# Layer 1 of the first image in the other stream, beside layer 0 of the second, with TensorE in order of emission

## The chip, the cores and the metric

The kernel runs on one core of a Trainium2 chip. The metric is the device time of one execution in microseconds, lower is better; where several runs are named, their median stands for them.

The engines, as the profile names them: PE is TensorE's matrix multiplication, PEld its loading of weights, DVE is VectorE, ACT is ScalarE, POOL is GpSimd, SP is SyncE, which here only issues transfers. ACT and POOL issue transfers too.

## The reference, cut to what matters

Four images of 48 channels and 256 x 256 pixels, in float32, go through four layers. Each layer normalises its input by groups of three channels and adds its result to its input (`_gn` is that normalisation):

```python
x = x + _L0_conv_ref(_gn(x), ...)   # 1x1 conv to 288, 3x3 depthwise conv, q*k in the spectrum of 8x8 patches,
                                    # layer norm over 96 channels, times v, 1x1 conv to 48
x = x + _L1_conv_ref(_gn(x), ...)   # 1x1 conv to 288, a filter in the spectrum of 8x8 patches, 3x3 depthwise conv,
                                    # gelu(first half) * second half, 1x1 conv to 48
x = x + _L2_conv_ref(_gn(x), ...)   # running sums over the image; two 3x3 convs give each pixel a box;
                                    # four bilinear look-ups in the sums, divided by the area
x = x + _L3_conv_ref(_gn(x), ...)   # 1x1 conv to 192, 3x3 depthwise conv, gelu * gate, 1x1 conv to 48,
                                    # a filter in the spectrum of 8x8 patches
```

The images don't depend on each other. Within an image a layer needs the whole of the layer before, because the statistics of the normalisation run over the image.

## The kernel before

**Two streams.** `Net.run` (L1354) holds two lists of jobs, a and b. A job is a generator that emits the instructions of one layer of one image piece by piece and yields a number after each piece, its cost in units of its own. `advance` takes the next piece from the stream whose sum of costs (`at`) is smaller, so the instructions of the two streams are emitted in turns. (n,i) is layer n of image i.

- a: the statistics of image 0, then (0,0), (1,0), (0,1), (1,1), (0,2), (1,2), (0,3), (1,3), then (3,0), (3,1), (3,2), (3,3).
- b: `patch_weights` (the matrices of layer 1), `taps` (the weights of layer 3), the statistics of images 1 to 3, then (2,0), (2,1), (2,2), (2,3).

A job waits until the layer before it of the same image is emitted in full, layer 1 also for `patch_weights`; the stream's sum is then raised to the time in units at which that was done. A layer 0 yields 1806 units, a layer 1 1425, a layer 2 3220, a layer 3 1080. So (1,0) has no partner: b has nothing to do until (2,0) may start.

**What belongs to a stream.** `self.stream` selects the PSUM banks (`bank`, L224: five of 512 float32 for a, two for b; layer 2 holds the eighth bank for its weights, L983, tag `w4`), the queue of ordinary transfers (`dma`, L227: SP for a, GpSimd for b) and the side of SBUF (`pool`, L234).

**Who sets the order on an engine.** The framework reorders the emitted instructions of an engine as it finds them ready, save those passed through `keep_in_program_order` (`pinned`, L230), which keep their order among each other. Pinned before the change: the first matmul of each group of layer 2 and its work on VectorE, the statistics of layers 0 and 1, and the transfers of layer 1's second and third phase, which are on SP by name whatever the stream.

**Layer 0** (`layer0`, L422) goes through 128 units. A unit is two rows of one half of the image; two units share a strip, for which `columns2` (L283) loads the input in six transfers (two buffers). The work on a unit is spread over several turns of the loop at L558: `convolve` (12 matmuls at L379 and 4 at L387 through `convolve2`, into four banks, evicted by ScalarE at L463), `spectra` (L471; L474, L477), `inverse` (L486, L487, L491), `gate`, `turn` (L524, L526), `project` (L536). Each turn yields twice, 7 units each time.

**Layer 1** (`layer1`, L655) has three phases. In the first it multiplies 16 strips by `win` (L692), 512 matmuls each into a bank of its own, evicts them (three of four on ScalarE at L699, one on VectorE at L697) and writes the result to DRAM as `hD`. In the second it goes through 36 groups of channels: `around` (L744) makes the rims of the patches (L750, into four banks) and sends them through small transfers (`yh` from `yb`, L761), and four times `gated` (L763) multiplies by `wd` and `yh` (L767, L773) into two banks, which L778 and L779 turn into the gated product; it goes to DRAM as `gD`. In the third it turns 16 strips of `gD` round (L844, three banks; evicted at L846), projects them (L856, one bank) and adds the input (L861). It yields 3 units for four matmuls in the first phase, 4 for a `gated` or an `around` in the second, 5 for a quarter of a strip in the third.

**Layer 2** (`layer2`, L961) first makes the running sums (`sums`, L893; L926, L947) and then goes through 32 pieces in four steps each, and one turn more to finish. A step is 16 gathers of GpSimd (L1105) into one of three buffers, the weighing and adding of the gathered values on VectorE (L1117 to L1127), and in turns the convolutions of a later piece (L999, L1008, L1011), its small products (L1024) and the finishing of an earlier one (L1136, L1143). A step yields 22 units. Its columns are loaded through ScalarE's queue (`look`, L1013).

**Layer 3** (`layer3`, L1214) is a loop of 135 turns of 8 units, mostly L379, L387 and L1268.

Of the kernel before, what the change touches and what calls it, by code (L numbers as in the profile page):

```python
# [188 lines left out]
class Net:  # L189
    def __init__(self, ctx, tc, a, out):  # L190
# [6 lines left out]
        self.stream = "a"  # L197
# [26 lines left out]
    def bank(self):  # L224
        return self.banks[self.stream].tile([128, 512], F32, name=self.nm("ps"), tag="ps")

    def dma(self, out, of):  # L227
        (self.nc.sync if self.stream == "a" else self.nc.gpsimd).dma_start(out, of)  # L228

    def pinned(self, instruction):  # L230

        return self.tc.keep_in_program_order(instruction)

# [137 lines left out]
    def convolve2(self, AB, W, n, j, to):  # L371
# [5 lines left out]
        def full(q, b):  # L377
            for g in range(3):
                nc.tensor.matmul(  # L379
                    to(q, b), A[:, j + half * q, 128 * b + g : 128 * b + g + 128], W[:, g, :],  # L380
                    start=b == 0 and g == 0, stop=b == 1 and g == 2,
                )

        def tails(b):
            for q in range(2):
                p = slice(64 * q, 64 * q + 58)
                nc.tensor.matmul(  # L387
                    to(q, b), B[p, j, 128 * b : 128 * b + 128], W[p, 3, :], start=b == 1, stop=b == 0
                )
# [32 lines left out]
    def layer0(self, x, mr, y, xb):  # L422
        nc, a = self.nc, self.a
        st = self.stat.tile([112, 129, 6], F32, name=self.nm("st"), tag="st" + self.stream, bufs=1)
        with ExitStack() as ctx:
# [39 lines left out]
            def spectra(t):  # L465
                t.t = []
                for f, c in ((self.fq, 0), (self.fk, 96)):
                    banks = [self.bank() for _ in range(2)]
                    for h in range(2):
                        p = slice(64 * h, 64 * h + 64)  # L470
                        nc.tensor.matmul(v3(banks[h]), f[p], t.qkv[p, :, c : c + 96], start=True, stop=True)  # L471
# [7 lines left out]
            def inverse(t):  # L479
# [5 lines left out]
                for h in range(2):  # L485
                    nc.tensor.matmul(po[64 * h : 64 * h + 64, 0:384], self.back[:, 0:64], t.t[h][:], start=True, stop=True)  # L486
# [34 lines left out]
            def turn(t):  # L521
                pt = self.bank()
                for b in range(4):
                    nc.tensor.transpose(pt[:96, 128 * b : 128 * b + 128], t.un[:, b, :], self.ident[:])  # L524
# [3 lines left out]
            def project(t, other):  # L528
# [5 lines left out]
                for i, of in ((0, other), (1, t)):  # L534
                    n = 48 if i else 64
                    nc.tensor.matmul(pp[64 * i : 64 * i + n, :], pr[:, 0:n], of.u[:], start=True, stop=True)  # L536
# [118 lines left out]
    def layer1(self, x, mr, y):  # L655
# [4 lines left out]
        with ExitStack() as ctx:  # L660
# [25 lines left out]
            for s in range(NS):  # L686
                xt = xts[s % 3]
                hs = sb.tile([128, 8 * NG, 2, 16], F32, name="hs", tag="hs")
                for b in range(16):
                    for h in range(2):  # L690
                        ps = self.bank()
                        nc.tensor.matmul(  # L692
                            ps[:, :288], xt[64 * h : 64 * h + 49, 128 * b : 128 * b + 128],
                            win[64 * h : 64 * h + 49], start=True, stop=True,
                        )
# [12 lines left out]
        with ExitStack() as ctx:  # L708
# [35 lines left out]
            def around(t):  # L744

                for e in range(4):
                    ps = self.bank()
                    for i in range(2):
                        c = 4 * i + e
                        nc.tensor.matmul(  # L750
                            ps[64 * i : 64 * i + 64, :].rearrange("p (s n) -> p s n", n=32),
                            t.wr[:, 64 * c : 64 * c + 64], t.hg[:, :, c, :], start=True, stop=True,
                        )
# [9 lines left out]
            def gated(t, e):  # L763
                both = [self.bank() for _ in range(2)]
                for i in range(2):
                    c = 4 * i + e
                    nc.tensor.matmul(  # L767
                        both[i][:].rearrange("p (s n) -> p s n", n=32), t.wd[:, 128 * c : 128 * c + 128],
                        t.hg[:, :, c, :], start=True, stop=False,
                    )  # L770
                for i in range(2):
                    p = slice(64 * i, 64 * i + 64)
                    nc.tensor.matmul(  # L773
                        order(both[i][:]), t.wd[p, 1024 + 128 * e : 1152 + 128 * e], pick(t.yh, e)[p],
                        start=False, stop=True,
                    )
# [32 lines left out]
        with ExitStack() as ctx:  # L809
# [25 lines left out]
            def turn(s, j):  # L835
                gs, got = strips[s], []
                for q in range(3):
                    pt = self.bank()
                    for b in range(4):
# [4 lines left out]
                        nc.tensor.transpose(pt[:96, 128 * b : 128 * b + 128], of, self.ident[:])  # L844
# [5 lines left out]
            def project(s, j, got):  # L850
                xt, yt = buffers[s % 2]
                pp = self.bank()
                for last in range(2):
                    for h in range(2):
                        n = 48 if h else 64
                        nc.tensor.matmul(  # L856
                            pp[64 * h : 64 * h + n, :], pr[:, h if last else 2, 0:n], got[2 if last else h][:],
                            start=not last, stop=bool(last),
                        )
# [494 lines left out]
    def run(self, layers=(0, 1, 2, 3)):  # L1354
# [5 lines left out]
        a = [("first", 0)] + [(n, i) for i in images for n in (0, 1) if n in layers] + [(3, i) for i in images if 3 in layers]  # L1360
        b = ([("weights", 0)] if 1 in layers else []) + ([("taps", 0)] if 3 in layers else [])
        b += [("first", i) for i in images[1:]]
# [9 lines left out]
        def advance(f):  # L1372
            self.stream = f
            if now[f] is None:
# [6 lines left out]
                now[f] = self.first_statistics(i) if n == "first" else self.patch_weights() if n == "weights" else self.taps() if n == "taps" else self.layer(n, i)  # L1381
            try:
# [74 lines left out]
```

## Time and profile before

The median of nine runs is 22818.67 us (22727.34 to 22904.18). The profiled execution took 22756.06 us; its span, from first to last instruction, is 22754.3 us, and the mean granted clock of TensorE is 0.854 of full speed.

| | busy us | share of the span | instructions |
|---|---|---|---|
| profiled execution (span 22754.3 us) | | | 227410 |
| PE | 18541.1 | 81% | 79706 |
| PEld | 11053.8 | 49% | 79706 |
| DVE | 10282.4 | 45% | 22561 |
| ACT | 6017.6 | 26% | 12781 |
| POOL | 8473.3 | 37% | 8902 |

Where the jobs lie in the span, read from the stretches in which their lines have instructions:

| us | stream a | stream b |
|---|---|---|
| 0 to 1890 | statistics of image 0, (0,0) | until about 1130: matrices of layer 1, weights of layer 3, statistics of images 1 to 3 |
| 1890 to 3080 | (1,0) | nothing |
| 3080 to 7550 | (0,1), (1,1) | (2,0): sums until about 3480, then gathers |
| 7550 to 12170 | (0,2), (1,2) | (2,1) |
| 12170 to 16750 | (0,3), (1,3) | (2,2) |
| 16750 to 21730 | (3,0), (3,1), (3,2) | (2,3) |
| 21730 to 22754 | (3,3) | nothing |

How to read it: a stretch of the span is printed as its bounds, its length, the busy time and the number of instructions of PE, PEld, DVE, ACT and POOL, the granted clock of TensorE (1.00 is full speed), the mean busy share of the sixteen DMA engines and the GB/s that they moved. A group of instructions is printed with its line, engine, operation and shapes, its count, its busy time in us and the mean ns of one. A float32 matmul stands in the records as two instructions, so 12 matmuls at L379 are 24 records. A wait names who waited, for whom, and the total, the number and the longest in us.

### The profile page before, as it was taken

The page shows a single profiled execution, that of the slowest core. Times are in us where ns is not written, and L with a number is a line of the kernel's source. Part 1 is how long each engine was busy: PE and PEld are TensorE (multiplying, and loading weights), DVE is VectorE, ACT ScalarE, POOL GpSimd, SP SyncE. Part 2 cuts the span into 40 slices and gives each one's busy share as a digit, 9 for nine tenths or more (in the row PEclk, how much of TensorE's full clock was granted, in tenths as well). Part 3 has the DMA queues.
Part 4 walks back from the last instruction along what each step waited for, and adds up shares of the span by engine and source line. Part 5 has one row for each costly group of instructions (what it writes and reads, how often), then busy time and mean ns, then how long its engine had stood idle before and what let it go on. Part 6 is the DMA issues. An engine that isn't in the chain of part 4 may idle for free.

```text
span 22754.3 us, 227410 instructions
## 1 busy us (share of the span) xinstructions
PE 18541.1 (81%) x79706; PEld 11053.8 (49%) x79706; DVE 10282.4 (45%) x22561; ACT 6017.6 (26%) x12781; POOL 8473.3 (37%) x8902
## 2 busy tenths in 40 slices
PE   9998898787777977777778777777788877877899
PEld 4564254444422544443225444442256666656688
DVE  4643244555444545554445455544442443333421
ACT  3445143332411333324113233241121111111112
POOL 1100004555454145544442455544422444444400
PEclk9998998888688988886889888868888888878899
DMA  6626863333787633337776333367764444444433
GB/s 175 159 60 226 278 194 96 99 105 99 229 258 234 182 94 98 99 91 232 253 233 185 94 100 96 96 209 248 239 196 113 109 109 107 106 102 105 109 85 77
DMA packets 1721733, 3401.42 MB, mean 149 GB/s; under 512 B 497086, under 2 KB 1270523, under 8 KB 1599832
## 3 DMA queue, kind: packets, MB, share of 16 engines
q1 hardware_dynamic: 1188976, 2092.38, 30.6%
q0 software_dynamic: 447648, 1097.85, 17.9%
q10 hardware_dynamic: 83968, 196.64, 3.3%
q8 instruction: 634, 10.39, 0.2%
q14 instruction: 507, 4.15, 0.1%
HBM read 2419.31 MB, written 831.99 MB: 143 GB/s over the span
## 4 chain that ended last, share of the span: by engine, by line
PE 63%; issue 10%; another core or an unknown queue 9%; DMA 8%; DVE 6%; ACT 2%; POOL 1%; SPq 1%; ACTq 1%; DVEq 0%; POOLq 0%
PE ps L379 22%; PE ps L999 5%; PE ps L387 4%; PE ps L692 4%; PE ps L471 4%; PE ps L767 2%; PE ps L1024 2%; PE ps L1268 2%; PE ps L773 2%; PE ps L750 2%; PE ps L856 2%; PE ps L486 2%; PE ps L844 1%; DMA yh<-yb 1%
## 5 line engine op out<-in xcount | busy, mean ns | idle before, releaser
L1105 POOL DMA_INDIRECT V<-t,idx x8192 | 8056.1, 983 | 8232.9 <-DVE res L1127 4296.9
L379 PE MATMUL ps<-W,A 128*128 128x288 f32 (+1 forms) x24576 | 6017.6, 394 | 720.4 <-issue 480.2
L379 PEld LDWEIGHTS ps<-W,A 128*128 128x128 f32 x24576 | 4563.2, 203 | 2094.5 <-issue 1167.9
L1125 DVE TENSOR_TENSOR V<-V 128x1536 f32<-128x1536 f32 (+3 forms) x2048 | 1817.3, 887 | 9.2
L1117 DVE TENSOR_TENSOR V<-V,w 128x1536 f32<-128x1536 f32 x1024 | 1764.8, 1746 | 47.6 <-DMA V<-t,idx 31.3
L463 ACT COPY qkv<-ps 128x288 f32<-128x288 f32 x2048 | 757.7, 401 | 3445.4 <-PE ps L387 1094.8
L999 PE MATMUL ps<-A,W 128*96 128x512 f32 x3072 | 1617.4, 665 | 62.3 <-issue 61.6
L1248 DVE TENSOR_TENSOR gp<-gl,ps 128x192 f32<-128x192 f32 x1024 | 350.8, 352 | 2654.1 <-ACT gl L1247 2117.5
L491 DVE BATCH_NORM_STATS2 bs<-o 128x6 f32<-128x96 f32 x2048 | 381.7, 247 | 2471.8 <-ACT o L487 1957.4
L767 PE MATMUL ps<-hg,wd 128*128 128x512 f32 x2304 | 1223.6, 652 | 309.2 <-issue 108.2
L692 PE MATMUL ps<-win,xt 49*128 49x288 f32 x4096 | 1123.9, 599 | 377.7 <-ACT hs L699 195.0
L387 PE MATMUL ps<-W,B 58*128 58x288 f32 (+1 forms) x8192 | 1251.7, 404 | 220.0 <-issue 154.3
L471 PE MATMUL ps<-qkv,c_dft_sb 64*128 64x384 f32 x4096 | 1064.8, 559 | 441.4 <-ACT qkv L463 247.5
L1247 ACT ACTIVATE gl<-ps 128x192 f32<-128x192 f32 x1024 | 331.0, 331 | 3706.1 <-PE ps L379 1945.2
L228 POOL DMA_DIRECT2D X<-x x96 | 72.7, 758 | 2978.6 <-issue 1977.7
L779 DVE TENSOR_TENSOR hg<-gl,ps 128x512 f32<-128x512 f32 x576 | 394.7, 685 | 1554.2 <-ACT gl L778 868.3
L692 PEld LDWEIGHTS ps<-win,xt 49*128 49x128 f32 x4096 | 681.7, 264 | 796.6 <-ACT hs L699 376.9
L699 ACT COPY hs<-ps 128x288 f32<-128x288 f32 x1536 | 851.9, 677 | 807.6 <-PE ps L692 560.3
L387 PEld LDWEIGHTS ps<-W,B 58*128 58x128 f32 x8192 | 742.6, 194 | 649.7 <-issue 515.5
L999 PEld LDWEIGHTS ps<-A,W 128*96 128x96 f32 x3072 | 519.9, 182 | 1051.3 <-issue 1042.0
L773 PE MATMUL ps<-yh,wd 64*128 64x512 f32 x2304 | 741.1, 718 | 254.1 <-DMA yh<-yb 128.3
L778 ACT ACTIVATE gl<-ps 128x512 f32<-128x512 f32 x576 | 342.0, 597 | 2204.0 <-PE ps L773 1373.1
(195 smaller groups left out, 21719.3 us busy)
## 6 DMA issues: line engine op xcount, KB each, us to landing
hg<-hD SPq DMA_DIRECT2D x144, 2048.0 KB
hD<-hs SPq DMA_DIRECT2D x60, 4608.0 KB
gD<-hg SPq DMA_DIRECT2D x144, 1024.0 KB
gs<-gD SPq DMA_DIRECT2D x64, 2304.0 KB
V<-t,idx POOLq DMA_INDIRECT x8192
xt<-b SPq DMA_DIRECT2D x128, 896.0 KB
wd<-wD SPq DMA_DIRECT2D x144, 768.0 KB
A<-x SPq DMA_DIRECT2D x256, 387.0 KB
```

What stands on the lines that cost most here:

```text
L379: nc.tensor.matmul(to(q, b), A[:, j + half * q, 128 * b + g : 128 * b + g + 128], W[:, g, :], start=b == 0 and g == 0, stop=b == 1 and g == 2,
L387: nc.tensor.matmul(to(q, b), B[p, j, 128 * b : 128 * b + 128], W[p, 3, :], start=b == 1, stop=b == 0)
L463: nc.scalar.copy(t.qkv[:, 2 * q + b, :], banks[2 * b + q][:, 0:288])
L471: nc.tensor.matmul(v3(banks[h]), f[p], t.qkv[p, :, c : c + 96], start=True, stop=True)
L692: nc.tensor.matmul(ps[:, :288], xt[64 * h : 64 * h + 49, 128 * b : 128 * b + 128], win[64 * h : 64 * h + 49], start=True, stop=True,)
L699: nc.scalar.copy(hs[:, :, h, b], ps[:, :288])
L767: nc.tensor.matmul(both[i][:].rearrange("p (s n) -> p s n", n=32), t.wd[:, 128 * c : 128 * c + 128], t.hg[:, :, c, :], start=True, stop=False,
L773: nc.tensor.matmul(order(both[i][:]), t.wd[p, 1024 + 128 * e : 1152 + 128 * e], pick(t.yh, e)[p], start=False, stop=True,)
L999: m = nc.tensor.matmul(to[q], W[:, g, :], A[:, 2 * q : 2 * q + 2, g : g + 256], start=q == 0 and g == 0, stop=q == 1 and g == 2,)
L1105: nc.gpsimd.indirect_dma_start(out=V[:, k, 4 * cr : 4 * cr + 4, :].rearrange("p e c -> p (e c)"), out_offset=None, in_=table, in_offset=ba ...
L1117: self.pinned(nc.vector.tensor_mul(Vm, Vm, wm.unsqueeze(2).to_broadcast([128, 32, 48])))
L1125: self.pinned(nc.vector.tensor_add(V[:, :, 0:n, :], V[:, :, 0:n, :], V[:, :, n : 2 * n, :]))
```

## The change

(1,0) leaves a's list and stands in b's list after the statistics and before (2,0). So a goes on with (0,1) when (0,0) is emitted, and b emits (1,0) at the same time. The costs that (1,0) yields are halved, so that two units of it are emitted for one of a; those of layer 2 are multiplied by 0.96.

While (1,0) is being emitted the net is `crossed`. Then
- the ordinary transfers change places: those of a (layer 0) go to GpSimd's queue, those of b (layer 1) to SP's;
- `bank` gives b a third bank in every third turn, the one that layer 2 holds later for its weights (tag `w4`); a keeps its five;
- every matmul and transpose of layers 0 and 1 passes through the new `pe`, which pins it, so TensorE keeps the order of emission of both streams together. Outside the crossing `pe` changes nothing.

The diff, cut: the other calls of `nc.tensor` in layers 0 and 1 are wrapped in `self.pe(...)` in the same way.

```diff
@@ -194,7 +194,7 @@
-        self.stream = "a"
+        self.stream, self.crossed, self.turns = "a", False, 0
@@ -222,14 +222,21 @@
     def bank(self):
+        if self.crossed and self.stream == "b":
+            self.turns += 1
+            if self.turns % 3 == 0:
+                return self.banks["b"].tile([128, 512], F32, name=self.nm("ps"), tag="w4", bufs=1)
         return self.banks[self.stream].tile([128, 512], F32, name=self.nm("ps"), tag="ps")
 
     def dma(self, out, of):
-        (self.nc.sync if self.stream == "a" else self.nc.gpsimd).dma_start(out, of)
+        (self.nc.sync if (self.stream == "a") != self.crossed else self.nc.gpsimd).dma_start(out, of)
...
+    def pe(self, instruction):
+        return self.pinned(instruction) if self.crossed else instruction
@@ -376,17 +383,17 @@
-                nc.tensor.matmul(
+                self.pe(nc.tensor.matmul(
                     to(q, b), A[:, j + half * q, 128 * b + g : 128 * b + g + 128], W[:, g, :],
                     start=b == 0 and g == 0, stop=b == 1 and g == 2,
-                )
+                ))
...
@@ -1357,9 +1364,13 @@
-        a = [("first", 0)] + [(n, i) for i in images for n in (0, 1) if n in layers] + [(3, i) for i in images if 3 in layers]
+        early = (1, 0) if 1 in layers and len(images) > 1 else None
+        a = [("first", 0)] + [(n, i) for i in images for n in (0, 1) if n in layers and (n, i) != early]
+        a += [(3, i) for i in images if 3 in layers]
+        pace = {(2, i): 0.96 for i in images}
+        pace[early] = 0.5
         b = ([("weights", 0)] if 1 in layers else []) + ([("taps", 0)] if 3 in layers else [])
-        b += [("first", i) for i in images[1:]]
+        b += [("first", i) for i in images[1:]] + ([early] if early else [])
         b += [(2, i) for i in images if 2 in layers]
@@ -1379,8 +1390,9 @@
+            self.crossed = todo["b"][:1] == [early] and now["b"] is not None
             try:
-                at[f] += next(now[f])
+                at[f] += next(now[f]) * pace.get(todo[f][0], 1)
```

## The prediction, made before the run

> **What bounds the kernel now.** I first read the slices of the span (569 us each; POOL is busy only where layer 2 gathers), then the busy time of stretches that hold one stage each. Layer n of image i is written (n,i); L379 is a line.
>
> ```profile
> PE   9998898787777977777778777777788877877899
> POOL 1100004555454145544442455544422444444400
> PEclk9998998888688988886889888868888888878899
> ```
>
> Before the gathers and after them TensorE is full or nearly so; in between it is seven or eight tenths busy at a lower clock, and GpSimd never more than half.
>
> ```profile
> core 0: us, PE busy (x) PEld busy (x) DVE busy (x) ACT busy (x) POOL busy (x), PEclk, DMA share, GB/s
> 0.00:1130.00 1130.00, 1028.65 (x4066) 556.51 (x4067) 619.38 (x2062) 416.59 (x946) 161.55 (x272) 0.95 0.65 168
> 1200.00:1700.00 500.00, 500.00 (x2350) 303.06 (x2349) 212.82 (x678) 235.16 (x587) 0.00 (x0) 1.00 0.20 58
> 1885.00:2140.00 255.00, 207.25 (x1009) 144.51 (x1011) 81.50 (x127) 195.19 (x376) 0.00 (x0) 0.78 0.97 327
> 2140.00:2830.00 690.00, 592.69 (x1749) 190.81 (x1745) 156.73 (x222) 135.06 (x226) 0.00 (x0) 0.94 0.85 277
> 2830.00:3080.00 250.00, 226.56 (x1328) 127.34 (x1328) 95.53 (x224) 104.27 (x202) 3.02 (x4) 0.94 0.83 276
> ```
>
> Row 1 is (0,0) beside the other stream's set-up, row 2 (0,0) alone. The last three are the phases of (1,0), which runs alone for 1195 us: 1026.5 us of TensorE work, 168 us idle. (0,1) has no convolution before 3080.
>
> ```profile
> 3600.00:5500.00 1900.00, 1534.25 (x5935) 860.02 (x5934) 1061.91 (x2486) 599.79 (x1333) 1003.34 (x1012) 0.86 0.38 101
> 5750.00:6250.00 500.00, 362.10 (x1156) 199.99 (x1154) 230.94 (x395) 198.11 (x346) 244.18 (x255) 0.64 0.73 235
> 6350.00:7000.00 650.00, 504.32 (x1481) 171.98 (x1480) 307.30 (x511) 94.87 (x159) 330.31 (x345) 0.88 0.79 250
> 17400.00:21400.00 4000.00, 3172.41 (x16875) 2524.99 (x16874) 1579.14 (x2960) 507.88 (x1172) 1795.68 (x1889) 0.83 0.43 106
> ```
>
> These are layer 2 beside layer 0, layer 1's first and second phase, and layer 3. L1105 alone has 984, 247, 333 and 1835 gathers there. A step of layer 2 is 16 gathers; with two like stretches for each of the later images a step takes 31.8, 31.5, 31.1 and 34.9 us, and TensorE idles 6.6, 7.9, 6.8 and 7.2 us of it. The idle time hardly depends on the companion: it belongs to layer 2. The timeline shows one such hole:
>
> ```profile
> 4000.96 0.58 ACTq L295 DMA_DIRECT2D B<-x  x1
> 4011.83 0.68 ACT L1011 ACTIVATE hm<-ps,b 96x512 f32<-96x512 f32 x1 [14.70 <-remote]
> 4018.47 1.97 PE L536 MATMUL ps<-u,pr 96*64 96x512 f32 x4 [22.46 <-issue]
> ```
>
> ScalarE, which also issues layer 2's loads, stands still until the burst of gathers ends, and TensorE waits 22 us for it. 512 steps at about 7 us are 3600 of the 4213 us that TensorE idles in all. So I read the time as TensorE's work plus idle time fixed by layer 2's steps plus what is idle elsewhere.
>
> **The change, part by part.** In the units that the generators yield, (0,1) costs 1806 and (1,0) 1425, halved to 712.5 by its pace. Both start at 1918; when (1,0) ends, 102 half units, 51 units, of (0,1) are emitted. Then layer 2 begins, at pace 0.96, with 1094 units of (0,1) left.
>
> *The joint stretch.* Layer 1's matmuls: 1026.5 us less 6.1 of layer 2's (L926). Its first phase ran at clock 0.78; at 0.95, the clock of row 1, 207 become 170, so 983. Layer 0: row 2 has 1130 records of L379, 24 a unit, 47.1 units in 500 us, 10.62 us each; 51 units are 542. Together 1525 us of TensorE. How full it will be is not in the trace; the nearest row is row 1, two streams without layer 2: 1028.65 of 1130, 0.91, giving 1675 us. The ends: 1.00 (row 2), 1525; 0.79 (4436 of 5600 us in the three stretches of layer 0 beside layer 2), 1930. I take 0.91. Against 1195: **+480**.
>
> That 0.91 holds what the new order brings. Every matmul of the two layers now stands behind the one emitted before it; where a layer 1 matmul waits for a bank or a transfer, layer 0's matmuls wait too, and behind them ScalarE's and VectorE's evictions of layer 0. Alone, (1,0) waited as follows (total, times, longest):
>
> ```profile
> PE ps L692 <- ACT hs L699: 38.8, 13, 5.8
> PE ps L773 <- DMA yh<-yb: 35.5, 19, 3.8
> PE ps L750 <- DMA wr<-wD: 31.5, 12, 24.6
> PE ps L844 <- DMA gs<-gD: 17.5, 1, 17.5
> ```
>
> The waits between phases (24.6, 17.5) stay, as nothing is emitted between; the 19 short ones for yh get shorter, with half a unit of layer 0 (5.3 us) about every third or fourth yield. Layer 1 rotates three banks where it had five.
>
> The Trainium skill ("Perfetto Trace Analysis", Optimizing Tensor Performance) has independent matmul groups rotate through different banks so that one's eviction overlaps the next one's matmuls, which speaks against going from five to three. No row here shows three banks; by the rule the low end, 1930 us and +735, would stand in place of +480.
>
> Moved transfers: layer 0's loads go to POOL's queue, 25.5 strips of 6 and some 12 block loads and stores, 165 issues at 0.54 to 0.76 us (L228's rows), 89 to 125 us of GpSimd, which is 0.00 busy in those slices: nothing. If that cover were gone the loads would be late and TensorE would wait at L379, as in row 1's stretch, where two A loads cost 32.8 us; that is in 0.91. Layer 1's transfers stay on SP's queue, which carried nothing else there. Bandwidth: 343 MB in 1195 us plus 58 GB/s for 542 us (31 MB) is 223 GB/s over 1675 us, under the 287 of now.
>
> *Taken from beside layer 2.* 51 units of (0,1). Its six matmul groups sum to 523.5 us for 47.1 units alone and 1321.1 us for 101.2 units from 3500 to 5500, 11.1 against 13.1 us: the unit there costs 10.62 x 1.174 = 12.5 us. As the idle time of a step doesn't follow the companion, all of it is saved: **-636**. The other end, 10.62 us, -542, holds if the slower clock belongs to the holes and stays. I take 12.5, the row of the place that the work leaves.
>
> The granted clock is 0.50 in the 50 us from 8010 that are mostly hole and 1.00 in the full 50 us from 7710. The Trainium skill ("TensorE: Matmul & The Clock Gate", Part 1) says that an idle window halves the clock and a busy one restores it. By that rule the loss sticks to the holes, so -542 would stand in place of -636, and the sum would be 94 us higher.
>
> *The end.* (3,2) is now emitted 144 before (2,3) ends; at 0.96 these are 150 units of layer 2, 6.8 steps of 22, alone. A step alone can't beat its gathers, 1.25 us from start to start, 20 us; the sum holds 12.4 for it (7 idle, 5.4 of layer 2's matmuls: 2752.8 us of L999, L1008, L1024 and L1136 over 512 steps). **+52**.
>
> *Starts.* Today layer 2 and the other stream's next layer start together; the 100 us from 7560, 100 from 12150 and 50 from 16800 hold 82 us of idle TensorE. The new starts lie apart. Between -82 (gone) and +82 (each stream dips by itself) I take **-30**, as a lone start finds the other stream's work. The extra pinning calls and the bank counter cost no instruction.
>
> Sum: 480 - 636 + 52 - 30 = **-134 us**. The profiled execution took 22756 us (span 22754), 62.6 below the median of the runs; from the median, 22818.7 - 134 = **22685**, 0.6% faster. A measurement of this kernel can tell about 0.3%, 68 us, from no change.
>
> **Rivals.** *Filled up*: TensorE is as full as in row 2, the joint stretch takes 1525: -284, 22535. For it: 168 us of waits that layer 0 could cover; against: the order can't choose the covering work.
>
> *The clock stays with the holes*: -542, sum -40, 22779, no change. For it: 0.50 and 1.00 above; against: L379 takes 445 ns in the mean there, 412 alone, more than a few slow matmuls after each hole.
>
> *Three banks in strict order* (slower): place, the joint stretch; (1,0) takes 512 + 432 + 256 = 1200 banks. If each costs half an eviction (0.60 to 0.69 us at L699, L778, L779), 0.32 us, TensorE idles 385 us instead of 150: 1910 us, +101, **22920**. It cancels the gain from 0.24 us a bank on and is slower from 0.29. For it: ScalarE, 195 of 255 us busy in phase one, also gets layer 0's 5 us a unit (235 us for 47.1). Against: 38.8 us of such waits for 512 evictions today.
>
> *The step keeps its length* (slower): beside layer 1's first phase TensorE works 23.7 us a step against 25.2 beside layer 0, and the step is only 0.3 us shorter. Were half the saving lost this way, 636 becomes 318: +184, 23003. Against: beside layer 3, 2.4 us more work makes it 3.1 longer.
>
> **How the numbers follow.** Forecast 0.36 (its own range 22620 to 22750), filled up 0.12, clock 0.16, three banks 0.22, step 0.14. Faster 0.48, same 0.16, slower 0.36. Low end: 22535 with another 52 from the starts (-82) and some of the tail, 22450. High end: 23003 and part of the clock's 94, 23050.
>
> **What would show it.** Layer 2's first load near 3560 instead of 3080; TensorE about 0.91 busy from 1885 to there, at 0.95; steps still with 6.6 to 7.9 us of idle TensorE; the last gather near 21600 instead of 21730; about 1000 us after it, as now. Many waits of L692, L767 or L844 for evictions would speak for the three banks, steps of an unchanged 31 to 35 us with less of (0,1) in them for the last rival. The prediction is wrong if the joint stretch exceeds 1810 us or layer 2's span shrinks by less than 500.

## The result

The changed kernel takes 22990.74 us (median of 15 runs, 22921.23 to 23052.45), the kernel before 22803.86 us (median of 46, 22705.32 to 22904.18). The ratio is 1.0084, 95% interval 1.0072 to 1.0095: 187 us slower, where 134 us less were forecast. The profiled execution took 23133.64 us (span 23131.8 us, mean granted clock 0.843). It lies 143 us above its median and that of before 48 us below, so the two profiles overstate the loss. Totals are taken from the medians below, and the place of an event, as the first gather, from the one profiled execution of each kernel.

The slices of the changed kernel's page, 578 us each:

```profile
PE   8999999776776787777777877777778877777779
POOL 1100001455454514445455145544541444444420
PEclk9997999886887898877888988768889888888889
```

The full stretch ahead of the gathers is longer and fuller than before, but its fourth slice, with TensorE at 9, was granted only 0.7. Behind it there are 7s and few 8s at the same clock: the thinner companion has left room, not time.

The joint stretch by layer 1's three phases, up to the first load of layer 2, in the changed kernel (PE busy after bounds and length, near the end the clock, the DMA share and GB/s):

```profile
1885.00:2360.00 475.00, 468.31 (x1577) 303.13 (x1576) 121.56 (x262) 266.10 (x503) 18.64 (x36) 0.70 0.55 181
2360.00:3230.00 870.00, 816.90 (x2944) 341.81 (x2943) 268.90 (x588) 289.38 (x561) 44.16 (x85) 0.97 0.71 234
3230.00:3640.00 410.00, 389.18 (x2029) 212.62 (x2027) 152.25 (x389) 175.47 (x370) 16.68 (x33) 0.98 0.60 191
```

TensorE is 0.95 busy over the 1755 us, 81 us idle in all. So nothing waits much here; the work itself takes 1674 us, 468 of them in a first phase at clock 0.70.

Next the whole span, cut where the gathers begin and end. First the kernel before, then the changed one:

```profile
0.00:3455.00 3455.00, 3149.90 (x13150) 1682.02 (x13150) 1444.99 (x4151) 1338.01 (x2952) 190.89 (x318) 0.94 0.61 182
3455.00:21709.00 18254.00, 14372.67 (x59620) 8450.11 (x59620) 8610.62 (x17927) 4467.72 (x9333) 8280.89 (x8582) 0.83 0.51 147
21709.00:22754.00 1045.00, 1018.52 (x6936) 921.63 (x6936) 226.77 (x485) 211.88 (x496) 1.48 (x3) 0.97 0.34 78
```

```profile
0.00:4005.00 4005.00, 3802.97 (x15648) 2076.68 (x15648) 1668.34 (x4873) 1641.26 (x3602) 280.59 (x492) 0.93 0.56 164
4005.00:22179.00 18174.00, 13919.59 (x57758) 8207.38 (x57758) 8429.01 (x17269) 4181.51 (x8710) 8252.10 (x8579) 0.82 0.51 147
22179.00:23131.00 952.00, 915.44 (x6300) 830.47 (x6300) 187.61 (x421) 191.06 (x450) 3.03 (x5) 0.98 0.34 79
```

The first gather comes 550 us later. Behind it TensorE has 556 us less to do (14372.67 + 1018.52 less 13919.59 + 915.44), but the time shrinks by 172 us only, in this pair of profiles. With the total from the medians it is 187 - 550 = -363 us. Either way the work went and part of the time stayed.

Between the first and the last gather TensorE idles 4255 us instead of 3881. Two groups by shape show where it waits longer (busy us and mean ns, then the idle time just ahead of the group and what ended it). Before:

```profile
L379 PE MATMUL ps<-W,A 128*128 128x192 f32 x12288 | 2524.4, 353 | 427.1 <-issue 297.0 <-DVE gp L1248 76.9 <-DMA A<-x 49.7
L471 PE MATMUL ps<-qkv,c_dft_sb 64*128 64x384 f32 x4096 | 1064.8, 559 | 441.4 <-ACT qkv L463 247.5 <-issue 193.6
```

The same two groups (layer 3's convolution, layer 0's spectra) in the changed kernel:

```profile
L386 PE MATMUL ps<-W,A 128*128 128x192 f32 x12288 | 2566.5, 356 | 517.8 <-issue 355.7 <-DVE gp L1255 130.9 <-DMA A<-x 28.6
L478 PE MATMUL ps<-qkv,c_dft_sb 64*128 64x384 f32 x4096 | 1080.9, 557 | 570.3 <-issue 310.6 <-ACT qkv L470 259.5
```

These two gained 220 us of idle time. It is not one new wait: the waits that were there got longer. A group doesn't tell beside which companion; the steps are sorted by that in the section on the prediction.

### The profile page after: what moved, and what is told of

It reads as the page before. It is cut to its first block, busy times and chain, and to the rows that moved or that the text cites. A ratio compares the mean times of both kernels' runs of the same rounds, so it can differ in the third digit from the quotient of the medians.

```text
span 23131.8 us, 227238 instructions
## 1 busy us (share of the span) xinstructions
PE 18638.0 (81%) x79706; PEld 11114.5 (48%) x79706; DVE 10285.0 (44%) x22561; ACT 6013.8 (26%) x12761; POOL 8535.7 (37%) x9075
## 5 line engine op out<-in xcount | busy, mean ns | idle before, releaser
L386 PE MATMUL ps<-W,A 128*128 128x288 f32 (+1 forms) x24576 | 6105.2, 397 | 773.2 <-issue 543.6
L386 PEld LDWEIGHTS ps<-W,A 128*128 128x128 f32 x24576 | 4608.5, 205 | 2209.9 <-issue 1233.6
L699 PE MATMUL ps<-win,xt 49*128 49x288 f32 x4096 | 1227.5, 634 | 405.3 <-ACT hs L706 172.3
L699 PEld LDWEIGHTS ps<-win,xt 49*128 49x128 f32 x4096 | 749.5, 273 | 850.3 <-ACT hs L706 375.7
L478 PEld LDWEIGHTS ps<-qkv,c_dft_sb 64*128 64x128 f32 x4096 | 451.4, 201 | 1089.2 <-issue 520.5
L774 PEld LDWEIGHTS ps<-hg,wd 128*128 128x128 f32 x2304 | 407.3, 199 | 1000.8 <-issue 638.7
```

The lines of the kernel that those rows point to most:

```text
L386: self.pe(nc.tensor.matmul(to(q, b), A[:, j + half * q, 128 * b + g : 128 * b + g + 128], W[:, g, :], start=b == 0 and g == 0, stop=b == 1 ...
L478: self.pe(nc.tensor.matmul(v3(banks[h]), f[p], t.qkv[p, :, c : c + 96], start=True, stop=True))
L699: self.pe(nc.tensor.matmul(ps[:, :288], xt[64 * h : 64 * h + 49, 128 * b : 128 * b + 128], win[64 * h : 64 * h + 49], start=True, stop=True,))
L774: self.pe(nc.tensor.matmul(both[i][:].rearrange("p (s n) -> p s n", n=32), t.wd[:, 128 * c : 128 * c + 128], t.hg[:, :, c, :], start=True, ...
```

## The experiments

The runs fell on at least five chips, of two kinds. On some the kernel before takes 22800 to 23130 us, on others 18200 us. So a ratio is always to the kernel before on the same chip, and "chip of 18200" or "of 22900" says which kind it was. The last section shows how the kinds differ.

**e1, e3, e15, e18: pace, order and the change itself on chips of 18200.** e1 and e15 are the kernel before with layer 2's pace alone (first diff); e3 is the changed kernel without the pinning (second diff); e18 is the changed kernel itself, to be read beside e15, which has the same pace (another chip of the same kind, where the kernel before takes 18199 and 18205 us).

```diff
-                at[f] += next(now[f])
+                at[f] += next(now[f]) * (0.96 if todo[f][0][0] == 2 else 1)
```

```diff
-        return self.pinned(instruction) if self.crossed else instruction
+        return instruction
```

> The kernel before with one edit: layer 2's costs times 0.96, so that stream a emits 21.1 units to a step of layer 2 instead of 22. Nothing else moves. Theory A (the length of a step of layer 2 does not follow its companion's work): the four gather stretches keep their sum of 16875 us, the last gather stays near 21725 us, and the 4% of stream a that is left over (518 of 12948 units) runs alone at the end, 518 x 0.95 us (1024 us for 1080 units of layer 3 alone) = 490 us: about 23290 us, ratio 1.021. Theory B (TensorE's work plus a fixed idle time, as the prediction had it): each step shortens by about 0.8 us (0.88 units at 12.5 us for 14), 400 us over 512 steps, last gather near 21320, ratio about 1.004.

> The changed kernel without the order of emission on TensorE: pe() hands its instruction on unpinned; streams, banks, queues and paces stay. With the pins the joint stretch from 1885 to layer 2's first load takes 1755 us with TensorE 0.95 busy. If strict order costs (rival of the prediction), the stretch falls to about 1600 us and the ratio from 1.008 to about 1.002. If the pins do nothing or help, it stays at 1755 or grows to 1850, ratio 1.008 to 1.013. The steps of layer 2 come after it and should not change under either.

> The kernel before with the pace of layer 2 at 0.96 alone, as in e1, which ran on a chip without standstills (1.0012 there). The pace gives each step of layer 2 4% less of its companion, about 1 us, and leaves that work, some 500 us, to the end, where it runs alone on a full TensorE. Theory K (steps keep their length): layer 2's span shrinks by half of the 500 us or less, 200 to 300 us more in all, ratio 1.009 to 1.013. Theory S (idle time fixed): the work only changes its place, ratio 0.998 to 1.003.

> The changed kernel itself on the chip of e16 and e17, so that its saving stands beside theirs. Where before takes about 22900 us, 1.008 again, with some 200 to 300 us of the 610 us that it takes from beside layer 2 come back as idle time. Where before takes about 18200 us: theory K, layer 2's gathers take as long as before there (13660 to 13690 us from the first to the last), and the joint stretch makes it 480 us longer less the shorter tail, ratio 1.02 or more; theory S, 1.000.

Measured: e1 1.0012 (1.0002 to 1.0023), e15 1.0008 (0.9999 to 1.0017), e3 1.0144 (1.012 to 1.0167), e18 1.0123 (1.0106 to 1.014), the last two on different chips. The pace costs next to nothing by itself there. Without the pins layer 2's first load starts at 3708 us instead of 3635 (e18), with 1762 us of TensorE's work in the joint stretch instead of 1668, and the first gather comes 45 us later. So the strict order costs nothing: it keeps layer 1 on time, and in the total it is worth 0.2% at most, within the two intervals. And the change loses on both kinds of chip. e18 against e15: first gather 571 us later, 583 us less of TensorE behind it, 386 us less time by the two profiles, 367 by the medians.

**e2: layer 2 alone.** The kernel before, in which layer 3 waits for (2,3).

```diff
- need = ... [("taps", 0)] if n == 3 else []
+ need = ... [("taps", 0), (2, images[-1])] if n == 3 else []
```

> The kernel before with one more condition: no layer 3 starts before (2,3) is done, so (2,3) runs without a companion and the four layers 3 run alone behind it. Theory A in its pure form: a step of (2,3) without a companion still takes 30 us or more, against 34.9 beside layer 3, and the gather stretch of (2,3) 3900 us or more (before: 4500). Theory B: the step falls to its own floor of about 20 to 21 us (16 gathers at 1.25 us), the stretch to about 2700 us. Something between, 24 to 28 us, would say that the step is set by a chain through ScalarE and VectorE in which the companion's instructions take part, but not by the amount of TensorE's work.

Measured: 19565.68 us (one run) beside 18207.18. It missed its aim: the framework pulled layer 3's unpinned matmuls forward into the stretch that was to be empty. What it left is one point, first the steps of (2,3) with little work beside them, then the same steps in e4 with all of layer 3 beside them:

```profile
14011.00:16791.00 2780.00, 1774.59 (x7961) 1321.46 (x7959) 1431.70 (x2596) 253.71 (x530) 2149.68 (x2105) 0.76 0.50 123
14079.00:17110.00 3031.00, 2992.10 (x19042) 2495.29 (x19042) 1752.97 (x3276) 591.07 (x1321) 2110.92 (x2108) 0.99 0.66 157
```

128 steps of 21.7 us with 13.9 us of TensorE work each, against 23.7 us with 23.4. Two us more for nine and a half of work: idle time isn't the same in every step, and 21.7 us is close to what the 16 gathers take one after the other (1.25 us from start to start, 20 us).

**e4, e10: layer 2's columns through SP instead of ScalarE**, against the standstills of ScalarE.

```diff
-  t.G[h] = self.columns2(x, 128 * t.i + 8 * t.s + 4 * h, 4, cols, nc.scalar.dma_start)
+  t.G[h] = self.columns2(x, 128 * t.i + 8 * t.s + 4 * h, 4, cols, nc.sync.dma_start)
```

> The kernel before with one edit: layer 2's columns are loaded through SP's queue instead of ScalarE's. Theory S (the idle 7 us of a step are ScalarE standing in the issue of these loads while the gathers run): TensorE's idle time per step falls below 4 us, a step from 31.8 to about 29 us beside layer 0 and from 34.9 to about 32 beside layer 3, the time by 1000 to 1500 us, ratio 0.93 to 0.96. Theory G (the hole is there whoever issues, because the loads or the gathers themselves are what is waited for): idle time per step stays at 6 to 8 us, ratio 0.99 to 1.02. Should SP's queue be held up by waits for the column buffers, the other stream's loads come late and the ratio lies above 1.02.

> The kernel before with layer 2's columns on SP's queue, once more, for a chip with the holes; on the chip with 18207 us, where there are none, it gave 0.994. Theory S (ScalarE stands in the issue of these loads while the gathers run): idle time of TensorE per step below 4 us, steps of 28 to 29 us beside layer 0, ratio 0.93 to 0.96. Theory G (the hole is there whoever issues): idle time 6 to 8 us, ratio 0.99 to 1.01.

Measured: e4 0.994 (0.9919 to 0.996, chip of 18200), e10 0.9963 (0.9946 to 0.998, chip of 22900). A small gain on both and the best version found, but not a cure: in e10 TensorE still idles 4245 us between the first and last gather (14400.97 us busy of 18646). The loads that ScalarE issues are not what stops it.

**e5, e6, e7: the pair again, and the changed kernel with layer 2's pace back at 1**, on one chip of 22900.

```diff
-        pace = {(2, i): 0.96 for i in images}
+        pace = {}
```

> The kernel before, unchanged, for its profile on the chip of these runs: the last four kernels ran on a chip on which the kernel before takes 18207 us instead of 22804, so their traces have no fitting partner. If that chip is met again: no holes of ScalarE during the gathers, steps of layer 2 near 23.5 us (16 gathers at 1.25 us and more), TensorE about 0.93 busy. On a chip like the first: 22750 us, steps of 31 to 35 us.

> The changed kernel, unchanged, beside the kernel before on the same chip. Theory A (the work taken from beside layer 2 is not returned, whatever holds the step) expects the joint stretch's cost nearly whole, 500 to 600 us, less 0 to 150: ratio 1.008 on a chip like the first, and 1.02 to 1.03 on one with 18207 us, where the gathers themselves hold the step at 23.5 us and TensorE's work beside them counts for nothing. Theory B (TensorE's work plus fixed idle time) expects the same few us of difference on both, ratio 0.995 to 1.005, and has to put the slowdown measured down to something else, as the pace of 0.96.

> The changed kernel with layer 2's pace back at 1, (1,0) still at 0.5. The last 660 units of layer 2, 30 steps, then have no companion. Theory A: 4 x 132 steps keep their length, whatever stream a does, so the last gather lies where the changed kernel has it, within 150 us, ratio to before within 0.005 of the changed kernel's. Theory P (the odd ratio 0.96 spoils the fit of the two streams' turns and is what lengthens the steps): steps fall back by 4% beside layers 0 and 3, the last gather 400 us or more earlier than in the changed kernel, ratio 0.02 lower.

Measured: e6 1.0075 (1.0046 to 1.0105), e7 1.0098 (1.0069 to 1.0128), e5 22846.16 beside 22867.58. In e7 stream a runs out first and layer 2's last steps have no companion. Two stretches of it, the lone end and layer 2 beside layer 0 and the first phase of layer 1:

```profile
21600.00:22050.00 450.00, 94.41 (x278) 44.34 (x277) 207.30 (x329) 10.85 (x15) 335.44 (x325) 0.57 0.33 86
4100.00:5500.00 1400.00, 1069.16 (x4037) 594.98 (x4038) 727.20 (x1662) 458.31 (x966) 659.25 (x672) 0.80 0.40 111
```

315 gathers start in the first, 19.7 steps of 22.9 us, with 18.1 us of TensorE idle in each; in the second 656 do, 41 steps with some 8 us (331 by 41). In the units of the generators layer 2 has 659 left when a is done, 30 steps; at 10 us more idle than an accompanied one that is 300 us. (In all, TensorE idles 4215 us between the gathers in e7 and 3987 in e5, 228 more.) At pace 0.96 those steps are spread, each step has about 4% less beside it, and the total is no better by a margin that the runs can tell. So the loss isn't in how the end is arranged.

**e8, e9: full rows in layer 1's first phase.** `win` sat twice in one tile, at rows 0 to 48 and 64 to 112, and each matmul used one half. Here each half gets a tile of its own whose other rows are zero, and all 113 rows are used; the result is the same. e8 is the kernel before with it, e9 the changed one.

```diff
-            win = w.tile([113, 288], F32, name="win")
+            wins = [w.tile([113, 288], F32, name=self.nm("win")) for _ in range(2)]
...
-                            ps[:, :288], xt[64 * h : 64 * h + 49, 128 * b : 128 * b + 128],
-                            win[64 * h : 64 * h + 49], start=True, stop=True,
+                            ps[:, :288], xt[0:113, 128 * b : 128 * b + 128],
+                            wins[h][:], start=True, stop=True,
```

> The kernel before with the first phase of layer 1 multiplying by 113 rows instead of 49: the weights of each half of the image stand in a tile of their own with zeros in the other rows, the result is the same. The granted clock of that phase was 0.78 in (1,0) alone, 0.63 beside layer 2 and 0.70 in the joint stretch although TensorE was 0.99 busy there. Theory R (the clock follows how many rows of the array work, not how long it is busy): the clock of the phase rises to 0.9 or more, its L692 matmuls shorten from 521 ns in the mean, unless two matmuls of 49 rows had run side by side, in which case the phase lengthens by up to a half of 255 us for each image: time between -1.0 and +1.5%. Theory I (idle gaps lower the clock): the clock stays below 0.8 in the phase.

> The changed kernel with layer 1's first phase on 113 rows. In the changed kernel that phase of the joint stretch (1885 to 2360) has TensorE 468 us busy at a granted clock of 0.70. Theory R (the clock follows the rows that work): the clock of those us rises to 0.9 or more, layer 0's matmuls there run at full speed, the phase shortens by 80 to 130 us, the joint stretch from 1755 to about 1650, the ratio from 1.0075 to 1.002 to 1.004. Theory I (the clock is low for another reason, or the phase is held by evictions): the stretch stays at 1755 and the ratio at 1.0075.

Measured: e8 0.9992 (0.9972 to 1.0013), e9 1.0032 (1.0015 to 1.0049). The phase alone, first before, then e8:

```profile
1890.00:2130.00 240.00, 198.80 (x972) 138.53 (x972) 78.18 (x121) 186.92 (x360) 0.00 (x0) 0.79 0.97 328
```

```profile
1890.00:2130.00 240.00, 237.62 (x965) 184.08 (x966) 78.78 (x120) 198.96 (x362) 0.00 (x0) 0.99 0.95 326
```

Alone, the phase gets the same number of matmuls done: before, TensorE isn't its bound (ScalarE is 187 of 240 us busy and the DMA 0.97), and with full rows TensorE is full as well. But the clock goes from 0.79 to 0.99. In the joint stretch TensorE is the bound, and there the clock counts. The two main groups between 1890 and 2340, first of the changed kernel, then of e9:

```profile
L699 PE MATMUL ps<-win,xt 49*128 49x288 f32 x928 | 288.9, 628 | 6.7 <-ACT hs L706 6.3
L386 PE MATMUL ps<-W,A 128*128 128x288 f32 x300 | 100.6, 497 | 0.0
```

```profile
L701 PE MATMUL ps<-win,xt 113*128 113x288 f32 x1016 | 266.1, 417 | 2.0 <-ACT hs L708 0.8
L386 PE MATMUL ps<-W,A 128*128 128x288 f32 x336 | 87.5, 410 | 0.0
```

Layer 0's own matmuls, unchanged in shape, fall from 497 to 410 ns beside neighbours that use more rows. The trace grants either the full clock or half of it: in the changed kernel these matmuls last 413 ns in the mean where it is full and 682 where it is half, and in e9 they all lie where it is full. The joint stretch ends 90 us earlier, at layer 2's first load at 3550 us instead of 3640 (the row runs 10 us on):

```profile
1885.00:3560.00 1675.00, 1597.39 (x6580) 792.22 (x6580) 546.72 (x1245) 720.64 (x1441) 82.94 (x159) 0.98 0.68 221
```

Now the first gather comes 482 us later than in e10, as was forecast, and the kernel is still 64 us (0.32%) slower than before: what stays of the miss lies behind the first gather.

**e11, e12: both edits**, in the kernel before and in the changed one.

> The kernel before with both: columns on SP's queue and 113 rows. If the two add, its ratio is that of the loads alone less 0 to 0.004 (113 rows alone: 0.9992).

> The changed kernel with both. Where ScalarE no longer stands in the gathers, a step should follow the companion's work more closely and the 51 units taken from it should come back: theory F (the step's floor from the holes is what kept the saving) expects it 0.003 to 0.008 below the kernel before with the same two edits. If the gathers themselves are the floor (23 us a step), it stays 0.005 or more above it.

Measured, on the chip of e9 and e10: e11 0.9976 (0.9959 to 0.9993), e12 0.9998 (0.9979 to 1.0017). The changed order is still behind, by 41 us, but less: the first gather comes 473 us later (3916 to 3443), and 432 of some 566 us of TensorE work behind it are saved.

**e13 and e16, e14 and e17: less and more work beside layer 2, and nothing else.** Less: layer 0 of images 1 to 3 leaves out the matmuls of the outer taps, so they are missing from its result. More: it does one matmul of each first bank twice. Both are cut: `later` is true from the second image on, and in the first the start and stop flags of the other matmuls follow.

```diff
         def tails(b):
+            if later:
+                return
```

```diff
         for q in range(2):
+            if later:
+                nc.tensor.matmul(to(q, 0), A[:, j + half * q, 0:128], W[:, 0, :], start=True, stop=True)
             full(q, 0)
```

> The kernel before, in which layer 0 of images 1 to 3 leaves out its matmuls of the outer taps (L387; the fourth part of the 3x3 convolution's taps is missing in its result, and B is loaded but not read). All of the removed work lies beside layer 2, nothing else is moved: 3072 records of 180 ns (145.1 us for 808 between 3500 and 5500), 551 us of TensorE. Theory S, the idle time of a step is fixed and removed work is saved in full: 551 us less, ratio 0.976. Theory K, a step of layer 2 keeps much of its length when its companion gets thinner, as the change showed (half of what it took away came back as idle time): 250 to 330 us less, ratio 0.985 to 0.989, and 220 to 300 us more idle TensorE between the first and the last gather. On a chip without the standstills of ScalarE (before near 18200 us) both say 3% less, 0.970.

> The kernel before, in which layer 0 of images 1 to 3 does the first matmul of each of its two first banks twice (the first result is overwritten, so the output is the reference's): 1536 more records of 294 ns (713.2 us for 2428 at L379 between 3500 and 5500), 451 us more of TensorE, all beside layer 2. Theory S: 451 us more, ratio 1.020. Theory K: part of it disappears in idle time that the step has anyway, 150 to 300 us more, ratio 1.007 to 1.013, and TensorE idles less between the gathers. If thin steps lose and full ones follow their work, K holds for the run with less work and S for this one.

> The kernel of e13 again (the outer taps of layer 0 left out for images 1 to 3), hoped to run on a chip with the standstills. Where before takes about 18200 us, 0.996 again. Where it takes about 22900 us: theory S (the idle time of a step is fixed), 551 us less, ratio 0.976; theory K (a step of layer 2 keeps much of its length when its companion gets thinner), half or less of it, 0.986 to 0.997, and 250 to 500 us more idle TensorE between the first and the last gather.

> The kernel of e14 again (1536 records more at L379 beside layer 2, the output the reference's). Where before takes about 18200 us, 1.019 again. Where it takes about 22900 us: theory S, 451 us more, 1.020; theory K with steps that are floored in both directions, 1.005 to 1.012; thin steps lose and full ones follow, 1.017 to 1.022.

Measured, all on chips of 18200: e13 0.9957 (0.9942 to 0.9973) and e16 0.9951 (0.9934 to 0.9968), 84 and 90 us less; e14 1.0187 (1.0172 to 1.0203) and e17 1.0168 (1.0151 to 1.0185), 340 and 312 us more. How much work that was is read from TensorE's busy time in the whole run, as a group's own busy time holds time that it shares with its neighbours. No profile of the kernel before was taken on such a chip; two others stand for it, e15 (16915 us, pace 0.96) and e4 (16791 us, pace 1, the loads on SP). e13 has 16404 us, 387 to 511 less, and saves about a fifth of it. e14 has 17201 us, 286 to 409 more, and it costs three quarters of it or more. The idle time says it best: 1320 us in e15, 1328 in e4, 1323 in e14, but 1688 in e13 and e16. Both theories' figures for such a chip were wrong for less work (0.970). One stretch beside layer 0 shows where the saving went, first e4, then e13:

```profile
3900.00:4900.00 1000.00, 978.43 (x4345) 564.17 (x4346) 773.98 (x1818) 441.57 (x972) 782.76 (x738) 0.99 0.55 142
3900.00:4900.00 1000.00, 892.27 (x3698) 524.36 (x3697) 753.15 (x1786) 442.43 (x962) 782.97 (x737) 0.94 0.51 131
```

With 86 us less of TensorE's work the 1000 us hold as many gathers, 714 and 713, a step every 22.4 us. In both GpSimd waits next to nothing for VectorE to free a buffer (1.2 and 0.3 us in all), and some 0.3 us lie between one gather and the next. So there the gathers are as long as TensorE's work, and taking work from TensorE alone saves nothing. In the same stretch of e14 TensorE is 987 us busy, and there are 682 gathers: more work does lengthen the step. The group of layer 0's convolution shows the room that was left as waits for layer 0's own products, first e15, then e13:

```profile
L379 PE MATMUL ps<-W,A 128*128 128x288 f32 x12288 | 3344.1, 421 | 30.0 <-DVE t L474 14.8 <-DMA A<-x 7.9 <-ACT t L477 7.1
L379 PE MATMUL ps<-W,A 128*128 128x288 f32 x12288 | 3280.5, 421 | 267.6 <-DVE t L477 194.5 <-ACT t L480 55.3 <-DMA A<-x 13.8
```

This isn't the changed kernel's case on a chip of 22900. There a step beside layer 0 takes over 30 us, and from the last gather of one step to the first of the next 13 to 14 us pass in the median, where 1.25 us lie between two starts within a step. Nor is it a like edit: the change takes whole units of layer 0, with their work on ScalarE and VectorE, and even on a chip of 18200 it saves 367 of 583 us (e18).

What such an edit saves on chips of 22900 wasn't seen, since neither pair fell on one.

## Why the prediction was wrong

The miss is 321 us, from -134 to +187. By the first gather it parts into 70 us ahead of it (+550 instead of +480) and 251 us behind it (-363 instead of -636 + 52 - 30 = -614).

**The step that failed: "As the idle time of a step doesn't follow the companion, all of it is saved: -636".** The removed work was sized fairly: 556 us in the first pair of profiles, 644 in e5 and e6, 566 in e11 and e12, 583 in e15 and e18, where the prediction had 542 and 636 as its two ends. But not all of it was saved. With the totals from the medians 363, 415, 432 and 367 us were, so 130 to 230 us came back as idle time, where the sum had 22. (The profiled executions alone give 71 to 384.) Layer 2's span, which was to shrink by 500 us or more, shrank by 80, 348, 409 and 236 us in these profiles.

The four stretches that the prediction rested on had like idle times (6.6 to 7.9 us), but like loads too, 23.6 to 27.7 us of TensorE work in a step; a row for a step with less of the same companion was not among them. The changed kernel gives it, as the pace takes some 4% of the companion out of every step. Here the steps are sorted by companion, those with over 95% of the companions' matmuls from one layer, for three pairs on chips of 22900: the mean length of a step and, in brackets, TensorE's idle time in it, first before the change, then after.

| beside | steps | before, changed | e5, e6 | e11, e12 |
|---|---|---|---|---|
| layer 0 | 204, 166 | 31.3 (6.8), 31.5 (7.7) | 31.8 (7.0), 30.9 (7.3) | 32.2 (7.4), 31.8 (8.0) |
| layer 1 | 171, 201 | 31.3 (7.4), 31.6 (8.3) | 31.3 (7.5), 31.4 (8.3) | 31.6 (7.7), 31.0 (7.7) |
| layer 3 | 126, 130 | 34.4 (7.2), 33.8 (7.3) | 34.6 (7.5), 33.8 (7.4) | 35.2 (7.8), 34.5 (7.8) |

(The counts are those of the first pair; the others differ by one or two.) Beside layer 3 the prediction's step held: the work fell by 0.6 to 0.7 us and the step with it. Beside layer 0 the work fell by 0.7 to 1.3 us, and a third of a us to 0.9 came back as idle time. Beside layer 1 the work fell by 0.5 to 0.7 us, and in two pairs of three the step didn't shrink at all. More steps lie beside layer 1 than before, too. With the pace back at 1 (e7) a step beside layer 0 idles 6.7 us and one beside layer 1 7.5, as before, and the idle time stands in the lone steps: a step with 4.8 us of work took 22.9. So the likeness of four rows showed a common load, not a law. What holds up the thinner steps on these chips was not found: it is not the gathers, which wait, nor the queue of layer 2's loads (e10).

**The rival "The step keeps its length" came nearest.** It gave 23003 us, but its size came out by a compensation, which is luck: it took half of the saving as lost (318 us), the medians show 130 to 230, and the joint stretch added 70. Its mechanism was seen beside layer 1 and in part beside layer 0, not beside layer 3. The argument against it, that 2.4 us more beside layer 3 made a step 3.1 longer, was an argument about more work, and about the one companion for which it holds. e13 and e14 show, on chips of 18200, that the two directions need not be alike: more cost three quarters or more, less saved about a fifth.

**The joint stretch: fullness underestimated, work too small.** TensorE was 0.95 busy, not 0.91, and the waits between phases and for banks stayed small. But 1525 us of work became 1674. The step "at 0.95, the clock of row 1, 207 become 170" failed: the first phase was granted 0.70, less than the 0.78 it had alone, though TensorE was 468 of 475 us busy. The prediction took the low clock for a result of idle time. The Trainium skill ("TensorE: Matmul & The Clock Gate", Part 1) ties the clock to idle and busy windows in the same way; here a phase that was 99% busy kept 0.70, and e8 and e9 raised it to 0.99 by using 113 rows instead of 49, so the measurement decides against both. With full rows the stretch takes 1665 us, close to the predicted 1675, with a first gather 482 us later than e10's (3918 to 3436) on the same chip. Even there the agreement is of the sum alone: 1590 us of work at 0.95, where 1525 at 0.91 were predicted.

**Three banks in strict order** fell. In the joint stretch of the changed kernel the waits for evictions were short:

```profile
PEld ps L699 <- ACT hs L706: 80.2, 243, 1.3
PEld ps L774 <- ACT gl L785: 50.5, 77, 1.8
```

They are waits of the weight loads, which overlap the matmuls; TensorE idled 81 us for all causes together, where the rival had 385. Three banks cost nothing that shows, though no run had another number of them. The prediction's reading of the rule on rotation as a case for 1930 us would have been 175 too long. The strict order wasn't a cost either (e3).

**The moved loads** were free: ahead of layer 0's L386 TensorE idled 0.0 us between 1890 and 2340, as its group shows above, and in the rest of the joint stretch too. **The clock stays with the holes**: the clock between the gathers was 0.83 and is 0.82, and the removed work, 556 to 644 us, covers the range between this rival's 542 and the forecast's 636, so it stays open. **The end**: a lone step has 18.1 us of idle time, not the 14.6 behind +52 (20 us less 5.4), and takes 22.9 us. For 6.8 such steps that would be 20 us more, a small part of the miss. **The tail** after the last gather shrank from 1045 to 952 us, where it was taken as unchanged; it went the good way. **The starts** (-30): TensorE's idle time in the steps over 80 us, which hold the sums of the next image, fell from 240 to 194 us (e5, e6: 254 to 194), the forecast's way.

## What to carry to other kernels

Work that is taken out from beside another stream can be worth less than its busy time, even where the engine is over 90% busy: look for what takes as long beside it (here a fixed number of gathers) and measure the saving by taking out a like amount, before paying for it elsewhere. A constant read from several stretches holds only over the loads that they span, and for each companion by itself. When two streams are joined, price the stretch by its work at the clock of its own shapes, and fill the rows before counting on a fuller engine.

## What the hardware showed that was not expected

**Chips differ by a quarter.** The changed kernel itself, on a chip of 22900 and on one of 18200 (e18): waits of GpSimd's gathers for their buffers, and of ScalarE for a releaser that the profile calls remote. On the first:

```profile
POOL V L1112 <- DVE res L1134: 4500.2, 287, 91.8
```

```profile
ACT gl L1254 <- remote: 1433.4, 122, 62.7
ACT qkv L470 <- remote: 899.1, 117, 33.1
```

On the second the gathers wait this long, and no wait of ScalarE is on a remote releaser at all:

```profile
POOL V L1112 <- DVE res L1134: 683.8, 102, 36.4
```

So the long holes that the prediction read as a property of layer 2 are absent there: TensorE is 0.91 busy from the first to the last gather (12272.78 of 13458 us) instead of 0.77, with gathers of 946 ns in the median on both. Where they occur, they survive when ScalarE's loads move to another queue (e10). What causes them was not found.

**The granted clock follows the shape of the matmuls.** 49 rows: 0.79 at 83% busy, 0.70 at 99% (with layer 0's matmuls between them); 113 rows: 0.99 at 99%, with no other change. The two halves of 49 rows also overlapped in time, which full rows give up (198.8 us busy become 237.6 for as many matmuls); the runs don't part the two.
